# A fused attention and mixture-of-experts kernel: another order for VectorE's routing work inside the attention loop

## The chip, the cores and the metric

The kernel runs on one core of one Trainium2 chip. The core has five engines with a queue each: TensorE (PE in the profile; its weight loads are PEld), VectorE (DVE), ScalarE (ACT), GpSimd (POOL) and SyncE (SP), which here issues most of the transfers. Each engine works through its own instructions in the order in which they are written; the engines meet only at semaphores. The metric is the device time of one execution in microseconds (us), lower is better. The kernel before took 3224.88 us (median of 3 runs, 3223.79 to 3228.11).

## The reference: what is computed

The input x has 8 batches of 1024 tokens of 512 features. All of it is float32.

1. Attention. LayerNorm of x, without scale or shift. Each of 16 heads has 32 features. With xh the normalized row, the angles are `theta_q = xh / (1 + |w_q|) + b_q + t * phi_q`, likewise `theta_k`, and `theta_v = xh / (1 + |w_v|) + b_v`, where t is the place of the token. Q and K are `concat(cos theta, sin theta)` (64 wide), V is `cos theta_v + sin theta_v`. Sine and cosine come from a table of 2048 entries with linear interpolation. Then causal softmax attention per head, and `theta_out = out / (1 + |w_out|) + b_out`; what is added to x is `cos theta_out + sin theta_out`.
2. Mixture of experts. LayerNorm again; a router, `softmax(xn @ Wr + br)` over 8 experts; each token goes to its best two experts; each expert takes from each batch the first 160 (`int(1024 / 8 * 1.25)`) of the tokens that chose it, in order of token; later ones are dropped. Each expert is 512 -> 2048 (relu) -> 512, and the outputs, weighted by the router's probabilities, are added to x.

The router therefore needs, for every batch: the row statistics of x after attention, the normalized rows, their product with Wr, the two largest probabilities of each token, and a running count of the tokens of each expert, which gives a token its slot.

## The kernel before, in words

**The attention loop.** The loop at L1736 runs n from 0 to 31: batch b = n // 4, and chunk c = n % 4, which is 4 of the 16 heads (128 features). A chunk has two pairs of heads. For each pair, `scores` (L675) makes ten tiles of scores by matmuls (L684, with a causal mask added by matmuls, L698), and ScalarE takes the exponential of each (L704). `attend` (L710) multiplies the exponentials by V (L718), and VectorE scales the result into `av_sb` (L726). `turn` (L742) transposes that back to token order on TensorE (L216), and VectorE divides by the row sums (`rec` L753, `o_p` L755). `o_pre` and `o_post` (L643, L651) make the output angle (L647, L438), its sine, the sum with x in the tile `x_mid` (L658), and the statistics of that sum (`st_mid`, L661).

**Work for the next chunk in the same iteration.** While a chunk's scores and products run, the angles of the next chunk are made. `qk_pre` (L508) transposes the normalized input on TensorE (L216) and VectorE forms the q and k angles (`qk_f`, L525); `angle` (L437) makes `qk_r` from it (L438). `square` (L440, L442) and `absolutes` (L581, L585) are ScalarE's work on these. In the middle of the iteration ScalarE does a block of sines: a table load, cos (L594), `sine` (L445) of q and k, of v and of the output angle, and then `nc.scalar.activation(warm, split_c, AF.Exp)` (L1844), which brings the table for the exponential back. I call the time from one of these L1844 instructions to the next a stage; a stage is the second half of one iteration and the first half of the next one. `qk_post` (L599) multiplies on VectorE (L448, `qk_c` and `qk_r`, 128x2048 each) and sends the pairs for the next scores by SP (L609). `v_pre` and `v_post` (L619, L639) do the same for v (L626, L631, L438, then L448 into `v`).

**The bank pairs.** Every tile `ps_s` is one of three pairs of PSUM banks: a tile of scores, the transposes of `turn` and `qk_pre`, and what the router puts into PSUM. TensorE can write the next tile only when the last reader of the pair's previous content is done. Exponentials release a pair on ScalarE; copies and sums release one on VectorE.

**The router of a batch.** `router(b)` (L787) is a generator. It runs through the four chunks of the batch after b, one step at a time, by `next(route)` or by `route_on(slot)` (L1755), which does it only in the chunk of that number. For all batches but the last its steps are

- places and root: eight aggregations of `st_mid` (L798) and the inverse root of the variances (`inverse_root`, L355: 12 small instructions L361 to L369); in the same step rows 0 and 1: two tiles of 128 tokens normalized (`rows`, L811, L813) and sent to DRAM by SP (L819)
- for each pair of row tiles g = 0 to 3: features (TensorE transposes the rows, L216, VectorE copies them to `xT`, L838), the next two rows (L813, with the store of `x_mid` at L792 after the last), and sums (products with Wr, L875; VectorE copies them to `lg`, L880; sums over chunks by L858; VectorE adds br into `prob`, L882)
- choice: the largest logit and its subtraction (L926, L927), an empty step, the exponential on ScalarE (L930), then division (L932 to L934) and the two best experts (L941 to L948, once each), then the mask and the sums over row tiles (L954 to L957)
- counts: TensorE counts the tokens before each (L858 on `mask` and `prior`), and VectorE reads the counts (L966, L967)
- slots (L970 to L982), with scatters by POOL after them.

**What sets the order.** The engines PE, DVE, ACT and SP are scheduled by hand (L121): an engine's order is the order of the calls in the loop body. `with_asides(count)` (L1759) advances the tiles of scores by `count`, and each side generator in `asides` by one step per tile. `part(route)` (L988) is the router up to its next named step. `residual` is `o_post` of the chunk before the last. `begin` is true in the second half of an iteration with c == 0 and the first half of that with c == 1. Seven routers (batches 0 to 6) run in the loop; the eighth runs among the experts, from `ending` (L1886), and is not touched. After the loop, the experts take from about 1300 us to the end.

## Time and profile before

| what | value |
|---|---|
| median of 3 runs | 3224.88 us (3223.79 to 3228.11) |
| the profiled execution's own time | 3227.77 us |
| its span, first to last instruction | 3226.0 us |
| PE busy | 3114.4 us, 97% |
| DVE busy | 2309.3 us, 72% |
| ACT busy | 1680.1 us, 52% |
| mean granted TensorE clock | 0.992 |
| window 205 to 1280 us (seven batches with a router) | 1075.0 us, of them PE busy 1021.14, ACT 856.70, DVE 831.25 |

The profile is of one execution. Busy time of an engine is the union of its instructions. A wait names the instruction that waited and the one whose end released it, as inferred from semaphores; a line such as `L684` is a line of the kernel. PEclk is the part of TensorE's full clock that was granted. A matmul's end is modelled, so a busy PE need not be at its peak.

### The profile page before, as it was taken

Reading aid. Unit: us, or ns where it says so; the run is one execution under the profiler, and the core shown is the slowest. Engines: PE = TensorE matmul, PEld = TensorE weight load, DVE = VectorE, ACT = ScalarE, POOL = GpSimd, SP = SyncE. Lnnn points to the kernel's source line nnn. Section 1 sums busy time; section 2 is a strip of 40 time slices with the busy share of each in tenths; the row PEclk is TensorE's granted clock in tenths of the full one; section 3 lists DMA queues with packets and bytes.
Section 4 is the critical chain, followed back from the end, with each engine's and each line's share of the span. In section 5 each row is a group of like instructions: output and inputs, shape, how many; then the busy total and the mean of one; then the engine's idle time right before and its main releaser. Section 6 shows DMA issues by size and latency. Waiting matters only on the chain.

```text
span 3226.0 us, 52455 instructions
## 1 busy us (share of the span) xinstructions
PE 3114.4 (97%) x20086; PEld 2155.2 (67%) x20086; DVE 2309.3 (72%) x4808; ACT 1680.1 (52%) x2630; POOL 420.0 (13%) x387
## 2 busy tenths in 40 slices
PE   5999999999999999999999999999999999999998
PEld 2544444444444444578788688689699699698697
DVE  8887878787877776646767767767767668657665
ACT  7878888878787876413323323323423423423423
POOL 2000202020202022421101101100110110110010
PEclk9999999999999999999999999999999999999999
DMA  5435354444544443434414514513523523523421
GB/s 165 145 99 164 102 161 112 151 131 137 159 140 133 116 132 92 131 83 115 136 41 115 147 33 112 153 29 110 154 37 102 153 47 94 151 57 105 128 53 27
DMA packets 288554, 358.80 MB, mean 111 GB/s; under 512 B 28376, under 2 KB 199088, under 8 KB 276272
## 3 DMA queue, kind: packets, MB, share of 16 engines
q1 hardware_dynamic: 264944, 312.20, 32.9%
q0 software_dynamic: 22912, 43.22, 7.1%
q8 instruction: 160, 2.62, 0.3%
q14 instruction: 90, 0.74, 0.1%
q10 hardware_dynamic: 448, 0.02, 0.0%
HBM read 207.02 MB, written 81.22 MB: 89 GB/s over the span
## 4 chain that ended last, share of the span: by engine, by line
PE 73%; DVE 11%; ACT 11%; issue 3%; DMA 1%; another core or an unknown queue 0%; SPq 0%; POOLq 0%; ACTq 0%; POOL 0%; DVEq 0%
PE ps_p L1238 30%; PE ps_p L1474 10%; PE ps_p L1537 10%; PE av L718 8%; PE ps_p L1352 8%; PE ps_s L684 7%; ACT e L704 6%; PE ps_s L216 1%; DVE st_mid L661 1%; ACT qk_c L594 1%; DVE av_sb L726 1%; ACT t_r L445 1%; ACT qk_r L445 1%; DVE qk_f L525 1%; DVE x_mid L658 1%
## 5 line engine op out<-in xcount | busy, mean ns | idle before, releaser
L684 PE MATMUL ps_s<-qk 64*128 64x512 f32 (+3 forms) x3072 | 598.2, 513 | 64.7 <-ACT e L704 23.6
L704 ACT ACTIVATE e<-ps_s 128x1024 f32<-128x1024 f32 (+1 forms) x640 | 559.1, 943 | 114.4 <-PE ps_s L698 53.9
L718 PE MATMUL av<-e,v 128*64 128x512 f32 (+3 forms) x3072 | 509.5, 488 | 0.0
L684 PEld LDWEIGHTS ps_s<-qk 64*128 64x128 f32 x3072 | 267.2, 191 | 256.6 <-ACT e L704 102.5
L718 PEld LDWEIGHTS av<-e,v 128*64 128x64 f32 x3072 | 206.0, 137 | 278.8 <-issue 258.6
L1238 PE MATMUL ps_p<-xe_s,t 128*128 128x256 f32 (+1 forms) x1024 | 319.1, 434 | 6.5 <-ACT hid L1248 6.5
L1238 PE MATMUL ps_p<-xe,w 128*128 128x256 f32 (+1 forms) x1024 | 317.6, 433 | 1.1 <-issue 1.1
L1238 PE MATMUL ps_p<-xe,t 128*128 128x256 f32 (+1 forms) x1024 | 318.0, 433 | 0.0
L1316 POOL DMA_INDIRECT out_dram<-y,slots x80 | 127.2, 1590 | 1262.4 <-ACT y L1311 1008.1
L769 POOL DMA_INDIRECT slot_d<-token,slot x128 | 153.8, 1202 | 1055.3 <-issue 658.9
L1238 PEld LDWEIGHTS ps_p<-xe_s,t 128*128 128x128 f32 x1024 | 194.8, 191 | 88.6 <-ACT hid L1248 7.1
L1238 PEld LDWEIGHTS ps_p<-xe,t 128*128 128x128 f32 x1024 | 194.6, 190 | 80.9 <-issue 1.3
L1238 PEld LDWEIGHTS ps_p<-xe,w 128*128 128x128 f32 x1024 | 193.7, 190 | 79.4 <-issue 1.2
L1537 PE MATMUL ps_p<-w_t,hid 128*128 128x256 f32 x960 | 212.4, 379 | 0.8 <-DVE y L1590 0.8
L1281 DVE TENSOR_TENSOR hid<-hid 128x256 f32<-128x256 f32 (+1 forms) x128 | 63.4, 495 | 207.4 <-ACT hid L1279 203.7
L1537 PEld LDWEIGHTS ps_p<-w_t,hid 128*128 128x128 f32 x960 | 180.0, 190 | 24.4 <-DVE y L1590 1.2
L1238 PE MATMUL ps_p<-xe_s,w 128*128 128x256 f32 (+1 forms) x512 | 158.9, 433 | 0.6 <-ACT p L1254 0.6
L726 DVE TENSOR_SCALAR av_sb<-av,inv_o 128x512 f32<-128x512 f32 x128 | 94.8, 745 | 84.8 <-PE av L718 80.7
L1352 PE MATMUL ps_p<-w,hid 128*128 128x256 f32 x640 | 142.9, 379 | 0.0
L1474 PE MATMUL ps_p<-w,hid 128*128 128x128 f32 x1104 | 141.8, 275 | 0.0
L1311 ACT ACTIVATE y<-y,slots 128x256 f32<-128x256 f32 (+1 forms) x120 | 65.9, 578 | 143.5 <-DVE y L1389 105.5
L698 PEld LDWEIGHTS <-keys_b 64*128 64x128 bf16 x1536 | 79.1, 95 | 90.6 <-issue 72.2
(291 smaller groups left out, 5231.6 us busy)
## 6 DMA issues: line engine op xcount, KB each, us to landing
w<-in_L_ffn_W_dram SPq DMA_DIRECT2D x256, 256.0 KB
w<-in_L_ffn_W_dram SPq DMA_DIRECT2D x64, 512.0 KB
qk<-qk_c SPq DMA_DIRECT2D x124, 256.0 KB
qk<-qk_r SPq DMA_DIRECT2D x120, 256.0 KB
qk_base<-base_d SPq DMA_DIRECT2D x28, 1024.0 KB
xn_d<-xn SPq DMA_DIRECT2D x72, 256.0 KB
rows_d<-xg SPq DMA_DIRECT2D x70, 256.0 KB
x_mid<-in_L_attn_x_dram SPq DMA_DIRECT2D x16, 1024.0 KB
```

Source lines behind the costliest of these rows:

```text
L684: nc.tensor.matmul(ps[:, a, at : at + w], lhsT=pair[r, 1, kb * P : (kb + 1) * P], rhs=pair[r, 0, q0 : q0 + w], start=at == 0, stop=not own ...
L698: nc.tensor.matmul(out_, lhsT=keys_b[r, part, :], rhs=late, start=False, stop=part == 1, skip_group_check=True,)
L704: nc.scalar.activation(e, ps[:, :, :n], AF.Exp, scale=UNIT * UNIT / math.sqrt(2 * DH))
L718: nc.tensor.matmul(av[a * 64 : (a + 1) * 64, q0 - 512 * h :], lhsT=vt[:, kb, 2 * pr + a, :], rhs=es[i][:, a, at : at + w], start=kb == 0, ...
L726: nc.vector.tensor_scalar(av_sb, av, inv_o[:, q : q + 1], None, ALU.mult)
L769: queued = nc.gpsimd.indirect_dma_start(out=slot_d[b], out_offset=bass.IndirectOffsetOnAxis(ap=idx, axis=0), in_=src, in_offset=None,)
L1238: nc.tensor.matmul(ps, lhsT=weights[:, k, :], rhs=rows[:, k, :], start=first and k == 0, stop=last and k == 1, skip_group_check=True,)
L1311: nc.scalar.activation(part, part, AF.Identity, scale=meta[:, e, jj[r], 1:2].bitcast(F32))
L1316: ins = nc.gpsimd.indirect_dma_start(out=out, out_offset=bass.IndirectOffsetOnAxis(ap=meta[:, e, jj[r], 0:1], axis=0), in_=y, in_offset=No ...
L1352: nc.tensor.matmul(ps, lhsT=hid[:, k, part, cols], rhs=ws[weight][:, k, :], start=first and k == 0, stop=last and k == NHQ - 1, skip_group ...
L1474: nc.tensor.matmul(ps, lhsT=left[:, k, :], rhs=right[:, k, :], start=first and k == 0, stop=k == 3, skip_group_check=True,)
L1537: nc.tensor.matmul(ps[:, b * DC : (b + 1) * DC], lhsT=hid[:, k, part, b * P : (b + 1) * P], rhs=ws[weight][:, k, :], start=first and k == ...
```

## The change

Nothing is computed that was not computed before: each engine has as many instructions as before, and the orders of SP's transfers and of POOL's work are the same. The order of calls in the loop body is another one.

- Places, root and rows 0 and 1: they stood at the end of the iteration with c == 0, on VectorE ahead of `qk_f` and `qk_r` of the next iteration. They now stand in the iteration with c == 1, after `qk_r`.
- v in the iteration with c == 1: `v_post` stood right after `qk_r`, followed by `v_pre` of the next chunk. `v_post` now stands after features 0 and rows 2 and 3, and `v_pre` after rows 4 and 5. v's square on ScalarE stood after five of the ten tiles of scores; it now stands after the ten, directly ahead of the sines.
- Features 0: their transposes on TensorE stood ahead of the first tile of scores of c == 1, and stand behind it.
- Choice, in the iteration with c == 2: `residual` (`o_post`, L448, L658, L661) stood after the first best expert, and now stands ahead of the whole choice. The exponential L930 stood after four tiles of scores and now stands after eight. The division, the two best experts and the sums over row tiles stood ahead of `turn` and `o_pre`, and now stand behind them.
- Sums 2 in c == 1 and counts in c == 2: VectorE's part stood behind the second product of `qk_post` (L448, `qk_r`), and stands ahead of it.

```diff
         if more:
             angle(*qk_st)
         if begin:
-            v_post(n, v_st)
-            v_st = rest(v_pre(n + 1))
+            next(route)
         if n and n + 2 < NCK:
             load_base(n + 2)
...
                 rest(keep(place, both(qk_st)))
             for h in range(2):
                 rest(attend(n - 1, 1, h, es1[h], halves1))
-        for _ in range(2):
-            route_on(1)
         route_on(2)
         with_asides(1)
         route_on(2)
-        if c == 2 and route is not None:
-            asides.append(part(route))
+        for _ in range(2):
+            route_on(1)
+        if begin:
+            v_post(n, v_st)
+        choice = part(route) if c == 2 and route is not None else iter(())
+        if c == 2:
+            rest(residual)
         with_asides(4)
         rest(residual)
         for _ in range(2):
...
         if n == 0:
             rest(keep(place, both(qk_st)))
             v_st = rest(v_pre(1))
-        if n == 0 or begin:
             square(v_st[0])
+        with_asides(1)
+        next(choice, None)
+        with_asides(1)
+        route_on(1)
+        if begin:
+            next(route)
+            v_st = rest(v_pre(n + 1))
+        with_asides(1)
+        some(2, choice)
         with_asides(2)
-        for _ in range(2):
-            route_on(1)
-        with_asides(3)
         for g in asides:
             rest(g)
...
         if late:
             turn(1, halves1, pos)
             o_st = o_pre(n - 1, pos)
+        if begin:
+            square(v_st[0])
+        rest(choice)
         for _ in range(2):
             route_on(1)
...
             next(post)
         some(NTT, *products)
+        route_on(1)
+        route_on(2)
         next_pairs = rest(post) if more else None
 
         es1, halves1 = [[], []], []
         ahead = [scores(pairs[1], h, es1[h]) for h in range(2)]
-        route_on(1)
-        route_on(2)
         some(3, *ahead)
         begin = c == 0 and late
...
         if begin:
             route = router(b - 1)
-            next(route)
         some(2, *ahead)
         route_on(1)
```

## The prediction

> **What bounds the kernel now.** I read the page's shares first, then busy times by stage, then the waits, then the timeline where they fall. TensorE is busy 97% of the span and the experts (from 1300 us) show no gap, so only the attention loop can give anything. Busy time by stage (columns: stretch, length, then busy us of PE, PEld, DVE, ACT, POOL, then PE clock, DMA share, GB/s), for one batch without and with router work:

> ```profile
> PE 3114.4 (97%) x20086; PEld 2155.2 (67%) x20086; DVE 2309.3 (72%) x4808; ACT 1680.1 (52%) x2630; POOL 420.0 (13%) x387
> ...
> 329.01:363.98 34.97, 34.81 (x290) 17.40 (x286) 30.73 (x58) 31.60 (x34) 14.20 (x11) 1.00 0.38 91
> 363.98:406.08 42.10, 38.64 (x386) 19.30 (x384) 34.34 (x70) 31.95 (x33) 7.67 (x9) 1.00 0.50 144
> 406.08:446.72 40.64, 39.85 (x397) 20.44 (x387) 29.61 (x64) 32.52 (x34) 0.00 (x0) 1.00 0.53 164
> 446.72:486.15 39.43, 36.47 (x288) 17.88 (x284) 31.12 (x68) 31.91 (x33) 1.20 (x1) 0.96 0.46 134
> 521.51:565.12 43.61, 40.15 (x386) 19.54 (x384) 34.18 (x70) 32.08 (x34) 7.24 (x9) 0.96 0.48 139
> 605.77:643.51 37.74, 34.77 (x288) 17.28 (x284) 30.94 (x68) 31.74 (x34) 1.01 (x1) 1.00 0.47 140
> ```

> Call them stage 0 (no router), 1, 2 and 3. In stage 0 PE has 0.16 us idle in 34.97: there it is the bound. In stages 1, 2 and 3 it is idle for 3.46, 0.79 and 2.96 us. None of the engines is full there, so these are waits for order. PE's waits and ACT's longest wait in 200 to 1250 us (total, times, longest) name them:

> ```profile
> PE ps_s L684 <- ACT e L704: 19.4, 22, 1.8
> PE ps_s L684 <- DVE tmp L966: 14.5, 7, 2.1
> PE ps_s L684 <- DVE xT L838: 8.0, 7, 1.2
> PE ps_s L684 <- DVE prob L882: 5.1, 8, 0.7
> ...
> ACT qk_f L442 <- DVE qk_r L438: 101.8, 26, 7.7
> ```

> The timeline (start, us, engine) shows how stages 1 and 3 come to stand:

> ```profile
> 376.30 2.72 DVE L525 SCALAR_TENSOR_TENSOR qk_f<-ps_s,inv_qk,qk_base 128x512 int32<-128x512 f32 x4
> 381.17 2.19 ACT L442 ACTIVATE qk_f<-qk_f,split_c 128x1024 f32<-128x1024 uint16 x2 [7.36 <-DVE qk_r L438]
> ...
> 386.21 0.70 PE L684 MATMUL ps_s<-qk 64*128 64x256 f32 x4 [1.51 <-ACT e L704]
> 388.14 1.99 PE L684 MATMUL ps_s<-qk 64*128 64x512 f32 x8 [1.14 <-DVE xT L838]
> ...
> 447.77 2.28 DVE L448 SCALAR_TENSOR_TENSOR qk_r<-qk_f,qk_r 128x2048 f32<-128x2048 f32 x1
> 447.89 0.70 PE L684 MATMUL ps_s<-qk 64*128 64x256 f32 x4 [0.74 <-ACT e L704]
> 449.96 0.21 DVE L966 TENSOR_TENSOR tmp<-hot,ps_s 128x64 f32<-128x64 f32 x1
> 450.74 5.83 PE L684 MATMUL ps_s<-qk 64*128 64x512 f32 x18 [2.07 <-DVE tmp L966]
> ...
> 450.89:454.30 3.41, 3.41 (x10) 1.37 (x12) 3.34 (x5) 1.02 (x1) 0.00 (x0) 0.50 0.99 255
> ```

> VectorE reaches `qk_f` late because places, root and rows stand ahead of it (371.95 to 376.30). ACT, in order, cannot square q and k before 381.17, so its exponentials come late and PE waits 1.51; then PE waits for the pair that `xT` holds (1.14). In stage 3 PE waits for the pair with the counts, which VectorE reads only behind `qk_r`'s product. The last row is a stretch with the clock at 0.50, right behind that wait.

> **Stage 1, walked with the durations of this batch.** I keep every duration and change only the order; times are those of the profile.

> - qk: PE's transposes end at 373.18 (372.46 + 0.72), so `qk_f` starts at 373.24 instead of 376.30. From `qk_f`'s start to `qk_r`'s end it is 4.84 (376.30 to 381.14): `qk_r` ends at 378.0, 3.1 earlier. ACT's squares and absolutes take 4.0: done at 382.1 instead of 385.2.
> - places, root, rows 0 and 1: 4.35 (371.95 to 376.30), now 378.0 to 382.4. Waiting behind them on DVE: two `av_sb` (1.40), to 383.8, then `xT`. PE's products end at 381.98, its first tile of scores at 382.98, features' transposes at 383.5; DVE copies `xT` 383.8 to 385.1 (before: to 388.09).
> - PE: second tile to 384.6; third needs the first exponential (383.05 to 384.07): free; fourth needs `xT`: 385.1 against 388.14, 3.0 earlier. The moved rows' DMAs: rows 0 and 1 go to DRAM by SP when written (382.4), and rows 2 and 3 reuse their buffers at 385.1, 2.7 later; before, it was 11.6 (376.4 to 388.0). Where they land is in no row; if it takes longer than 2.7, DVE waits for the rest, and since `lg` behind it is ready only 0.2 ahead of PE's sixth tile, PE waits nearly as long: 0 to about 2 us, of which I take 0. SP's and POOL's orders are the same; behind these DMAs on SP stands the base load (issued at 379.04, now about 383), whose data are wanted at about 414. From the fourth tile to the next products it was 9.84 (388.14 to 397.98), and 9.6 without its small waits: products at 394.75, 3.2 earlier.
> - v: `v_post` (1.21, to 387.3) is needed at 394.75. `v_pre` (1.29 + 1.23 + 0.69) follows rows 4 and 5 and ends at 395.5. v's square writes in place and waits for that: ACT, done with the tenth tile at 394.2, stands 1.3 us, with the sines queued behind it. Square 1.15, sines with both table loads 8.5 (397.79 to 406.28): the exponential's table is back at 405.1, against 406.28. The square used to run between exponentials, where ACT had time; here it is on ACT's chain, paid out of the 3.2. If v's angle is 1 us later, the next stage's first exponential is 1 us later.
> - Start of stage 2: products end at 402.7, sums' matmuls to 403.4, three tiles to 406.0. `prob` (L882) is read ahead of `qk_r`'s product, at 404.9, so the wait of 0.64 is gone; the fourth tile waits for the first exponential, 406.1. It was 410.09. **4.0 us per batch so far.**

> **Stage 2 to 3.** (In chunk 2 of batch 0, without a router, `o_post` moves ahead too; DVE has idle time there, and I cost it at nothing.) PE is the bound in the rest of stage 2, so all moves up by 4.0; I walk in the old times. `o_post` (4.1) runs 428.55 to 432.7, then L926 and L927 to 433.15. L930 on ACT, behind eight tiles, runs at about 435: no wait. `turn`'s transposes end at 436.66; `rec` to the output angle takes 2.88 (441.37 to 444.25): to 439.6 instead of 444.3. So ACT's wait of 0.99 ahead of the output's sine is gone, and the table is back 1 us earlier. The choice then takes 2.17 (432.28 to 434.45) + 2.85 (438.52 to 441.37), to 444.6. PE gets to the counts at 444.49: **an added wait of about 0.2**, with the scores behind it. Then on DVE `av_sb` 0.66, `qk_c` 2.20, `av_sb` 0.66, L966 to L966 0.72: counts read at 448.85. The tile that waited until 450.74 starts at 448.9; the wait of 0.74 is gone. `qk_r` is 1 us later than if counts stayed behind, but its scores are a half iteration away. **1.8 us.**

> Sum of waits: (4.0 + 1.8) x 7 batches = 41 us.

> **The clock.** Of the seven stages 1, four show PEclk below 1, and of the seven stages 3, five. The same stage with and without: 43.61 against 42.10 (1.5 us) and 39.43 against 37.74 (1.7). 4 x 1.5 + 5 x 1.7 = 14.5 us. [...] I follow the row, and take two thirds, 10 us, since a stretch of 1.1 us (447.8 to 448.9) stays: ends 0 and 14.5.

> Bounds of the whole: nothing, if the waits only move; at most all PE idle of stages 1 to 3 (3.46 + 0.79 + 2.96 = 7.2, x 7 = 50) and the clock, 65 us. Taken: 41 + 10 = 51 of the profiled 3227.8, which is 2.9 above the median; from the median of 3224.9 that is **3174 us**.

> **Rivals.**
> - The waits go but the clock drops go on at other waits: 41, **3184**. For it: drops come in only some batches with the same waits. Against: less idle time to set them off.
> - The gain of stage 1 is given back at the sines, since v's angle stands behind rows 4 and 5 and ACT waits for it. If 2.5 of 4.0 go, (1.5 + 1.8) x 7 = 23 and half of the clock, 5: **3197**. For it: ACT's order has no way round the square. Against: stage 2's first exponential waited 1.59 for PE, so ACT has some room.
> - The change does nothing for PE: each wait is replaced by one as long. **3225**. Against: DVE is at 34.3 of 42.1 us, with idle time to use.
> - Slower: the load of `x_mid` in stage 2. `o_post` needs it at 435.71 now, at 429.8 - 4.0 = 425.8 then. The DMA share is 1.02, 1.03 and 0.98 in 403:409, 409:418 and 418:427 and 0.05 after, so the load lands by about 427, and starts 1.8 earlier with the store ahead of it: 425.2, just in time. If it is d late, DVE's choice and L930 are late; ACT has 2 us, and past that the last exponentials and the sines wait with it. With 8 us (5.8 and the clock) to lose, it decides at d = 10; at d = 12 it costs 2 x 7: **3239**.

> **Chances.** As worked 0.52, clock stays 0.18, given back 0.16, nothing 0.04, slower 0.10. The sum is the likeliest, not a mean. A range of 3160 to 3203 holds the first three, with the greater clock gain at its low end. A measurement here can tell 0.2% (6.4 us) from no change: faster 0.86, within 0.04, slower 0.10.

> **What would show it.** Right: stage 1 near 41 us, stage 2 near 37 (its end moves with ACT's sines, 1 us more than PE), stage 3 near 37, the three together near 115 to 117 instead of 122.2; no wait of PE for `xT` (8.0) or `prob` (5.1); that for L966 from 14.5 to about 8; ACT's wait of 7.36 ahead of q's square near 4; a new wait of ACT for v's angle near 1.3; PEclk of 1.00 in most stages. Wrong: PE waits longer than 1 us at the counts, ACT's new wait over 2.5 us, or DVE standing at rows 2 and 3 or at L658 for a transfer.

## The result, and the profile after

The changed kernel takes 3179.84 us (median of 4 runs, 3179.05 to 3180.82), the kernel before beside it 3224.38 us: a ratio of 0.986 (95% interval 0.9843 to 0.9877). The forecast was 3174 us. The profiled execution of the changed kernel has a span of 3177.3 us, against 3226.0.

The first row is from the page; the others are the table of stretches of the changed kernel (length, then busy us of PE, PEld, DVE, ACT, POOL, then PE clock, DMA share, GB/s). The stages are those of the batch shown in the prediction: stages 0, 1, 2 and 3 in order, then the longest stage 1 of the seven.

```profile
PE 3096.0 (97%) x20086; PEld 2147.3 (68%) x20086; DVE 2310.1 (73%) x4808; ACT 1676.5 (53%) x2630; POOL 420.6 (13%) x387
...
318.96:354.21 35.25, 35.09 (x296) 17.60 (x290) 31.03 (x58) 31.79 (x34) 13.92 (x11) 1.00 0.36 90
354.21:396.20 41.99, 40.49 (x402) 20.27 (x398) 35.48 (x73) 32.19 (x33) 7.88 (x9) 1.00 0.51 151
396.20:432.93 36.73, 36.50 (x355) 18.61 (x353) 26.53 (x61) 31.92 (x35) 0.00 (x0) 1.00 0.56 174
432.93:470.01 37.08, 36.22 (x298) 18.46 (x294) 32.62 (x68) 31.85 (x34) 1.21 (x1) 1.00 0.48 143
809.22:855.68 46.46, 42.39 (x402) 20.86 (x398) 35.26 (x73) 32.29 (x33) 7.68 (x10) 0.96 0.58 170
```

PE's idle in stage 1 fell from 3.46 to 1.50 us, in stage 2 from 0.79 to 0.23, in stage 3 from 2.96 to 0.86. Stages 1 to 3 of this batch take 115.8 us together, against 122.2. A stage is cut where ScalarE ends its sines, so a gain of PE in stage 1 shows mostly in stage 2: over seven batches stage 1 lost 3.0 us in all, stage 2 27.0 and stage 3 13.0. The longest stage 1 has 4.07 us of idle, and its clock is 0.50 for 3.41 us (837.66 to 841.07).

The waits of the changed kernel in 200 to 1250 us (total, times, longest):

```profile
ACT qk_f L442 <- DVE qk_r L438: 89.2, 26, 4.9
DVE xn L813 <- DMA xn_d<-xn: 12.2, 10, 3.1
ACT v_p L442 <- DVE t_r L438: 8.6, 13, 0.9
...
PE ps_s L684 <- DVE tmp L966: 5.0, 7, 0.7
PE ps_s L684 <- DVE lg L880: 4.4, 6, 1.0
PE ps_s L684 <- ACT e L704: 3.9, 9, 0.5
PE ps_s L216 <- DVE xn L813: 2.6, 3, 1.0
PE ps_s L684 <- DVE xT L838: 1.5, 3, 0.6
PE ps_s L684 <- DVE prob L882: 0.7, 1, 0.7
```

PE's four large waits (19.4, 14.5, 8.0 and 5.1) are now 3.9, 5.0, 1.5 and 0.7. Two are new: for `lg` and for the rows of L813, 7.0 us together. The second row shows what is behind them: VectorE stands 12.2 us at L813, for the store that still reads the row tile's buffer. That is the wait that the prediction had bounded at 0 to 2 us and taken at 0.

The timeline of the batch at 354 us (start, us, engine), in the places that the prediction showed:

```profile
364.19 2.73 DVE L525 SCALAR_TENSOR_TENSOR qk_f<-ps_s,inv_qk,qk_base 128x512 int32<-128x512 f32 x4 [1.93 <-PE ps_s L216]
368.98 2.19 ACT L442 ACTIVATE qk_f<-qk_f,split_c 128x1024 f32<-128x1024 uint16 x2 [4.93 <-DVE qk_r L438]
375.96 1.99 PE L684 MATMUL ps_s<-qk 64*128 64x512 f32 x8 [0.50 <-DVE xT L838]
376.05 0.55 DVE L813 TENSOR_SCALAR xn<-x_mid,mv,rstd 128x512 f32<-128x512 f32 x1 [0.23 <-DMA xn_d<-xn]
377.28 0.55 DVE L813 TENSOR_SCALAR xn<-x_mid,mv,rstd 128x512 f32<-128x512 f32 x1 [0.69 <-DMA xn_d<-xn]
379.35 1.99 PE L684 MATMUL ps_s<-qk 64*128 64x512 f32 x8 [0.19 <-DVE lg L880]
...
436.02 0.22 DVE L966 TENSOR_TENSOR tmp<-hot,ps_s 128x64 f32<-128x64 f32 x1
436.29 1.56 PE L684 MATMUL ps_s<-qk 64*128 64x512 f32 x6 [0.62 <-DVE tmp L966]
436.41 2.28 DVE L448 SCALAR_TENSOR_TENSOR qk_r<-qk_f,qk_r 128x2048 f32<-128x2048 f32 x1
```

The wait of 1.51 for an exponential is gone, `xT` costs 0.50 instead of 1.14, and the counts are read ahead of `qk_r`'s product: the tile behind them stands 0.62, where it stood 0.74 and 2.07.

### The profile page after: what moved, and what is told of

The parts are those of the page before. It is cut to its first block, busy times and chain, and to the rows that moved or that the text cites. A ratio compares the mean times of both kernels' runs of the same rounds, so it can differ in the third digit from the quotient of the medians.

```text
span 3177.3 us, 52455 instructions
## 1 busy us (share of the span) xinstructions
PE 3096.0 (97%) x20086; PEld 2147.3 (68%) x20086; DVE 2310.1 (73%) x4808; ACT 1676.5 (53%) x2630; POOL 420.6 (13%) x387
## 4 chain that ended last, share of the span: by engine, by line
PE 78%; ACT 11%; DVE 7%; issue 2%; DMA 2%; SPq 0%; another core or an unknown queue 0%; POOLq 0%; POOL 0%; ACTq 0%; DVEq 0%
PE ps_p L1238 30%; PE ps_p L1474 10%; PE ps_p L1537 10%; PE ps_s L684 9%; PE av L718 9%; PE ps_p L1352 8%; ACT e L704 6%; PE ps_s L216 1%; ACT qk_c L594 1%; DMA xn_d<-xn 1%; ACT t_r L445 1%; ACT qk_r L445 1%; PE ps_s L698 1%; ACT L594 1%; DVE qk_f L525 1%
## 5 line engine op out<-in xcount | busy, mean ns | idle before, releaser
L684 PE MATMUL ps_s<-qk 64*128 64x512 f32 (+3 forms) x3072 | 584.1, 502 | 33.5 <-DMA qk<-qk_r 12.5
L704 ACT ACTIVATE e<-ps_s 128x1024 f32<-128x1024 f32 (+1 forms) x640 | 555.1, 944 | 85.6 <-PE ps_s L698 46.2
L684 PEld LDWEIGHTS ps_s<-qk 64*128 64x128 f32 x3072 | 261.4, 187 | 219.6 <-ACT e L704 93.1
L1537 PEld LDWEIGHTS ps_p<-w_t,hid 128*128 128x128 f32 x960 | 180.0, 190 | 24.4 <-DVE y L1590 1.2
```

The lines of the kernel that those rows point to most:

```text
L684: nc.tensor.matmul(ps[:, a, at : at + w], lhsT=pair[r, 1, kb * P : (kb + 1) * P], rhs=pair[r, 0, q0 : q0 + w], start=at == 0, stop=not own ...
L704: nc.scalar.activation(e, ps[:, :, :n], AF.Exp, scale=UNIT * UNIT / math.sqrt(2 * DH))
L1537: nc.tensor.matmul(ps[:, b * DC : (b + 1) * DC], lhsT=hid[:, k, part, b * P : (b + 1) * P], rhs=ws[weight][:, k, :], start=first and k == ...
```

## The experiments

My theory: the gain is PE's idle time that the change removes in stages 1 to 3, and the half-clock stretches that this idle had set off; what is missing from the forecast is the wait for the stores of rows. The rivals: one part makes the gain alone (stage 2 lost 27 us, which points at the choice); rows and counts work only together; the clock goes by something else than these idles.

All runs are compared by one account. The loop is measured from the start of the first stage 1 to the last of the L1844 instructions (205.60 to 1280.67 us before). Its length less PE's busy time is the idle; the half-clock time is counted in stretches of 3.41 us. For the kernel before, the changed one and the one called best below, the row of the loop reads:

```profile
205.60:1280.67 1075.07, 1021.21 (x9040) 510.69 (x9034) 830.96 (x1665) 856.78 (x890) 145.04 (x129) 0.98 0.47 134
```

```profile
203.60:1235.76 1032.16, 1006.25 (x9040) 505.32 (x9034) 829.62 (x1665) 853.32 (x890) 144.33 (x129) 1.00 0.49 140
```

```profile
205.60:1224.77 1019.17, 1003.16 (x9040) 503.71 (x9034) 828.72 (x1665) 852.60 (x890) 140.62 (x129) 1.00 0.49 142
```

PE has the same 9040 instructions in each; 1075.07 - 1021.21 = 53.86 us is idle before, 25.91 after, 16.01 in the last.

| kernel | time, us | ratio to before (95%) | loop | PE idle | half-clock stretches |
|---|---|---|---|---|---|
| before | 3224.4 | 1 | 1075.1 | 53.9 | 10 |
| changed | 3179.8 | 0.9860 (0.9843 to 0.9877) | 1032.2 | 25.9 | 1 |
| rows_only | 3212.3 | 0.9955 (0.9938 to 0.9972) | 1070.0 | 45.0 | 14 |
| choice_only | 3216.8 | 0.9971 (0.9961 to 0.9981) | 1063.2 | 47.1 | 5 |
| counts_only | 3196.8 | 0.9908 (0.9892 to 0.9925) | 1043.4 | 39.8 | 1 |
| rows_back | 3202.0 | 0.9933 (0.9916 to 0.9950) | 1050.3 | 35.6 | 7 |
| prob_back | 3185.9 | 0.9875 (0.9856 to 0.9895) | 1037.6 | 30.0 | 2 |
| counts_back | 3191.9 | 0.9894 (0.9874 to 0.9914) | 1039.8 | 32.0 | 1 |
| rows_buf | 3172.3 | 0.9837 (0.9820 to 0.9853) | 1027.0 | 21.5 | 1 |
| v_first | 3177.1 | 0.9847 (0.9831 to 0.9863) | 1025.0 | 20.7 | 0 |
| reads_3 | 3173.8 | 0.9868 (0.9853 to 0.9883) | 1032.5 | 25.9 | 2 |
| reads_5 | 3180.4 | 0.9888 (0.9873 to 0.9903) | 1045.6 | 30.7 | 7 |
| square_mid | 3212.9 | 0.9992 (0.9983 to 1.0000) | 1071.1 | 50.3 | 14 |
| best | 3162.6 | 0.9833 (0.9819 to 0.9846) | 1019.2 | 16.0 | 0 |

The ratios are to the kernel before on the same chip: 3224.8 us beside the three single parts and rows_buf, 3226.0 beside the three kernels ending in _back and v_first, 3215.9 beside the last four. In these last four the part behind the loop is 5 to 10 us shorter; compare them with the others by ratio and by loop. A half-clock stretch costs about 1.7 us (measured below). With that, the change of idle plus 1.7 per stretch gives the change of the loop to within 3.5 us for every kernel but one (-28.0 - 9 x 1.7 = -43.3 for the changed kernel, measured -42.9). The exception, square_mid, is 7 us off: idle that lies inside a stretch at half clock is counted twice, which may be the reason; that is not shown.

### One part alone

rows_only, on the kernel before (places, root, rows, and v with its square):

```diff
         if begin:
-            v_post(n, v_st)
-            v_st = rest(v_pre(n + 1))
+            next(route)
...
-        for _ in range(2):
-            route_on(1)
         route_on(2)
         with_asides(1)
         route_on(2)
+        for _ in range(2):
+            route_on(1)
+        if begin:
+            v_post(n, v_st)
...
+        route_on(1)
+        if begin:
+            next(route)
+            v_st = rest(v_pre(n + 1))
...
+        if begin:
+            square(v_st[0])
```

> One part alone: places, root and rows behind q and k's angle, v's angle spread over the iteration with its square beside the sines; choice and counts as before. Theory A (the prediction's steps: stage 1's waits are PE's own, worth 4.0 us in each of 7 batches, and the clock of stage 1 comes back, 4 x 1.5): 3224.4 - 28 - 6 = 3190; no wait of PE for xT in L838 beyond 1 to 2 us in all, and half-clock stretches in stage 3 stay (5 of 7). Theory B (stage 1's marks moved by only 3 us in all and stage 2's by 27, so the gain is made by the choice behind the output's sum, not by the rows): 3218 to 3224. Theory C (rows and counts act only together, because a gain of stage 1 is lost again at the counts' wait): 3205 or more.

choice_only, on the kernel before:

```diff
-        if c == 2 and route is not None:
-            asides.append(part(route))
+        choice = part(route) if c == 2 and route is not None else iter(())
+        if c == 2:
+            rest(residual)
         with_asides(4)
...
         with_asides(1)
+        next(choice, None)
...
         with_asides(1)
+        some(2, choice)
...
+        rest(choice)
```

> One part alone: in stage 2 the output's sum and statistics go ahead, and the choice is spread behind them; rows, v and counts as before. Theory A (this part only takes away ACT's wait of 0.99 ahead of the output's sine and, alone, moves the counts later): 0 to 7 us faster, 3217 to 3224. Theory B (stage 2's 27 us are made here): 3197 or less. A slower result would come from counts that are late: PE waiting for them over 1 us in stage 3.

counts_only, on the kernel before:

```diff
         some(NTT, *products)
+        route_on(1)
+        route_on(2)
         next_pairs = rest(post) if more else None
...
-        route_on(1)
-        route_on(2)
         some(3, *ahead)
```

> One part alone: the counts and their reading ahead of q and k's product; all else as before. Theory A (removes the tile's wait for L966 of 2.07 and the 0.74 ahead of it, in which the last idle of about 1 stays: 1.8 us in 7 batches, and 5 half-clock stretches of stage 3 at 1.7): 3224.4 - 12.6 - 8.5 = 3203; PE's total for L966 from 14.5 to 5 to 8, the half-clock stretches of stage 1 stay. Theory B (the waits go, the half-clock stretches stay at other places): 3212. Theory C (the product is the later one by as much as was won, and its scores wait): 3220 to 3226.

The size of the parts is not the one that I gave them. The rows, which I held for two thirds of the gain, make 12.5 us alone (against 3224.8), the choice 8.0 and the two lines of the counts 28.0. That stage 2 got shorter does not mean that the choice did it: the choice alone takes 7.7 us from stage 2, and counts and choice without the rows (rows_back, below) 14.0 of the 27.0.

For rows alone, theory C has the time (3205 or more) and the coupling right, but not the place: the wait at the counts stays as it was, and the gain is lost at `prob`. PE's waits:

```profile
PE ps_s L684 <- DVE tmp L966: 14.5, 7, 2.1
PE ps_s L684 <- DVE prob L882: 11.4, 8, 3.1
```

and the place with the longest:

```profile
877.20 0.33 PE L698 MATMUL ps_s<-later_b,keys_b 64*128 64x128 bf16 x4
880.66 0.70 PE L684 MATMUL ps_s<-qk 64*128 64x256 f32 x4 [3.12 <-DVE prob L882]
```

The wait for `xT` is gone (0.9 in all), but PE comes to the start of stage 2 earlier and stands there for `prob`, which VectorE still reads behind `qk_r`'s product: 11.4 us instead of 5.1. Part of what the rows win is lost 20 us later. On top of it all seven stages 3 have half-clock stretches, four of them twice as long (14 stretches against 10), with the same idle of 0.74 and 2.07 as before.

Counts alone removed 14.1 us of idle (theory A: 12.6), though PE's wait for L966 fell only to 10.4, where A had 5 to 8. They removed nine stretches instead of five, also in stage 1, whose idle of 1.4 to 1.6 and 1.15 stood unchanged. So the number of stretches is not a matter of the idle's length alone; this is taken up below.

### One part undone

rows_back is the kernel before with the edits of choice_only and counts_only together, so the changed kernel without its first part.

> The changed kernel with the first part undone: places, root, rows and v as before; choice and counts as changed. The first four runs gave a way to count: time of the loop = PE's work + PE's idle + about half of the time at clock 0.50. Theory A (count by idle): per batch 0.45 + 1.50 + 1.15 stay in stage 1 and 0.6 to 0.7 in stage 3, against 1.6 in the changed kernel's undisturbed batches, but without its 7 us of waits behind the stores of rows: 8 us more idle, and 0 to 5 half-clock stretches of stage 1 at 1.7, 3188 to 3197. Theory B (the prediction's sizes: the rows are worth 28 and 6): 3214. Theory C (a half-clock stretch follows where a window of 3.41 us, on a grid fixed within an execution, has 1.7 us or more of idle): every half-clock stretch of this run starts on one grid of 3.41, and behind windows with 1.7 or more.

prob_back, on the changed kernel:

```diff
-        route_on(1)
         route_on(2)
         next_pairs = rest(post) if more else None
...
+        route_on(1)
         some(3, *ahead)
```

> The changed kernel with one of the two moved lines undone: stage 2's sum, prob (L882), is read behind q and k's product again; the counts stay ahead of it. Theory A (this line, not the counts, is what rows alone lacked: there PE stood 11.4 us for prob): PE's wait for L882 is 7 to 20 us in all, 3188 to 3196. Theory B (the prediction's size, 0.64 in 7 batches): 3184. Theory C (no matter for PE): 3180.

counts_back moves the other of these two lines back (`route_on(2)`) and leaves `route_on(1)`.

> The changed kernel with the other moved line undone: the counts are written and read behind q and k's product again; prob stays ahead of it. Theory A (count by idle): 1.80 (choice alone) to 2.81 (before) of idle in stage 3 against 0.65, 8 to 15 us, and 0 to 7 half-clock stretches at 1.7, 3188 to 3206, PE's wait for L966 10 to 15 us. Theory B (with the choice late, the counts' place no longer matters): 3180 to 3183. Half-clock stretches, if any, on one grid of 3.41 us behind windows with 1.7 or more of idle.

In place, the rows are worth 18.2 us of the loop (1050.3 - 1032.2): 9.7 of idle and six stretches. Theory A had the idle right (8) and the stretches too low (7 in the run), so the time lies above its range; B's 34 is refuted. `prob`'s line is worth 5.4 and the counts' 7.6. PE's wait for L882 is 8.1 us in prob_back, in the range that A gave, and 0.7 with the line in place; the time, 3185.9 from two runs 7.7 us apart, is below A's range and between the two theories; the 0.64 per batch of the prediction is what the old order showed, not what leaving the line would cost in the new order. For the counts, A holds at its lower end: PE's wait for L966 is 10.6. The choice was not undone by itself in the full change, so what it is worth there is not known.

### The stores of rows

rows_buf, on the changed kernel (`bufs=3` also stands at the two other places that use these buffers, not shown):

```diff
-            xn = row2.tile([P, D], F32, name="xn2")
+            xn = row2.tile([P, D], F32, name="xn2", bufs=3)
...
+        work = row2.tile([P, 2 * P], F32, name="lg", bufs=1)
+        quarter = [
+            work[:, i * NTT * E : (i + 1) * NTT * E].rearrange("p (t e) -> p t e", e=E)
+            for i in range(4)
+        ]
...
-            oh = t3(f"hot_{k}")
+            oh = quarter[k]
...
-        mask, prior = t3("mask"), t3("prior")
+        mask, prior = quarter[2:]
```

> The changed kernel with three buffers instead of two for the router's row tiles; to make room, the tiles hot, mask and prior of the choice lie in the buffer of lg, and nothing else is changed. Theory A (rows 2 and 3 wait for the stores of rows 0 and 1; 12.2 us of VectorE, of which PE stands for L813 2.6 and for L880 4.4, and the one half-clock stretch of stage 1 hangs on it): 3179.8 - 7 - 1.7 = 3171, L813's wait for its store gone or under 2 us, PE's waits for xn and lg under 2 us together. Theory B (PE stands at this place for something else that is as late, the exponentials or features): 3177 to 3180 with the wait for the store gone. Theory C (the shared buffer adds a wait): above 3182.

v_first, on the changed kernel:

```diff
-        for _ in range(2):
-            route_on(1)
+        route_on(1)
         if begin:
             v_post(n, v_st)
+        route_on(1)
```

> The changed kernel with v's product (L448 into v, 1.21 us of VectorE) between features and rows 2 and 3 instead of behind rows 2 and 3; two buffers. Theory A (the stores of rows 0 and 1 need 2 to 3 us and the product covers 1.2 of it): VectorE's wait of L813 for stores from 12.2 to 3 to 6 us, PE's waits for L813 and L880 together from 7.0 to 2 to 4, 3173 to 3177. Theory B (rows 2 and 3 are late by the product instead, and PE's sixth tile waits for lg as long): 3179 to 3183.

In both, theory A has the cause right. The three lines are VectorE's wait for the stores in the changed kernel, in rows_buf and in v_first:

```profile
DVE xn L813 <- DMA xn_d<-xn: 12.2, 10, 3.1
```

```profile
DVE xn L813 <- DMA xn_d<-xn: 4.7, 3, 2.6
```

```profile
DVE xn L813 <- DMA xn_d<-xn: 3.1, 4, 1.1
```

PE's waits for L813 and L880 fall from 7.0 to 2.1 and to 0.2. I had expected under 2 us to remain of VectorE's wait in rows_buf; 4.7 did, since a third buffer serves row 2, and row 3 still takes row 0's. The half-clock stretch that was to go with the wait is still there in rows_buf and is gone in v_first. The loop is 5.2 and 7.1 us shorter. The intervals of the times overlap with each other and with that of the changed kernel; it is the waits and the loop that tell them apart.

### v's square

square_mid, on the changed kernel:

```diff
             v_st = rest(v_pre(n + 1))
+            square(v_st[0])
         with_asides(1)
...
-        if begin:
-            square(v_st[0])
```

> The changed kernel with v's square right behind v's angle, among the last exponentials, instead of beside the sines. Theory A (beside the sines it lies on ACT's chain with 1.15 and the wait of 0.9, and the middle has room): 1 to 2 us per batch faster, 3168 to 3175. Theory B (in the middle ACT stands for the angle, ready at 386.7 in the batch at 354 us, with three exponentials queued behind that were done by 385.9): PE waits for L704 with the products, 2 to 3 us per batch slower, 3194 to 3203.

Nearly the whole gain is gone (ratio 0.9992). The two lines are the waits that took its place:

```profile
PE ps_s L216 <- ACT e L704: 34.0, 34, 4.6
ACT v_p L442 <- DVE t_r L438: 32.8, 13, 4.8
```

ScalarE stands up to 4.8 us for v's angle, three exponentials are queued behind it, and PE stands for the bank pairs that they hold. Theory B holds, with twice its price: 24.4 us of idle, and 13 more half-clock stretches, which B had left out. So, with v's angle spread behind the rows, the square has to go behind the exponentials. The rival "given back at the sines" is answered by the changed kernel itself: there the wait is at most 0.9.

### The clock

In the kernel before, the half-clock stretches of the loop start at 229.02, 450.89, 546.46, 703.48, 768.33, 925.34, 1020.92, 1085.77 and 1242.78 us; the first is 6.83 us long, the others 3.41, and the granted clock in them is 0.50. One unit fits all the starts, 3.4133 us (1013.76 us from the first to the last, over 297): in it they stand at 0, 65.00, 93.00, 139.00, 158.00, 204.00, 232.00, 251.00 and 297.00 from the first. Below, a window is one such unit, on the grid that the stretches of an execution fix. How much idle in a window goes ahead of half clock, these starts do not say. Two kernels ask this, both from the changed kernel:

```diff
         for k in range(TOPK):
-            TT(tmp, hot[k], place, ALU.mult)
+            for _ in range(3 if k else 1):
+                TT(tmp, hot[k], place, ALU.mult)
```

> The changed kernel in which VectorE does each of the two reads of the counts (L966, 0.25 us from one to the next) three times, with the same result: PE's idle ahead of the tile that waits for them grows by 1.0, from 0.65 to 1.65 in one piece in each of 7 batches. Theory A (a half-clock stretch needs 1.7 us of idle in one window of the 3.41 us grid): no stretch at 0.50 in stage 3, cost 7 us, 3187. Theory B (any idle piece of over about 1 us can set it off): 4 to 5 stretches in stage 3, 3195.

reads_5 has 5 in place of 3.

> The same with five times each: idle 2.65 in one piece, nothing else changed. Theory A (1.7 us in one window of the grid): the two parts of 2.65 are both under 1.7 only where a window's border falls in the middle 0.75 of it, so about 78% of the stages, 5 to 6 of 7 (or all or fewer, where a batch is near a whole number of windows long), are followed by 3.4 us at 0.50: 14 + 5.5 x 1.7 = 23, 3203. [...]

The edit repeats only the second of the two reads (`if k`), not each of them as I had written: two and four more reads, 0.25 us from one to the next, not four and eight. So the idle came to 1.24 and 1.84 us (1.75 of it in one piece), not 1.65 and 2.65, and the times that the theories gave are too high. The question is answered all the same: reads_3 has no stretch in stage 3 (theory B, any piece of over about 1 us, had 4 to 5); reads_5 has five in seven (theory A had 5 to 6, for an idle of 2.65), and in its other two batches a border cuts the idle. Windows of the grid in reads_5: an idle of 1.84 that lies in one window and the window after it, then the idle of a batch in which a border cuts it:

```profile
284.27:287.68 3.41, 1.57 (x20) 1.05 (x18) 3.17 (x11) 2.10 (x3) 0.00 (x0) 1.00 0.45 86
287.68:291.09 3.41, 3.41 (x10) 1.39 (x10) 3.38 (x3) 1.02 (x1) 0.00 (x0) 0.50 0.98 231
...
745.07:748.48 3.41, 1.89 (x22) 1.11 (x18) 3.24 (x8) 2.54 (x3) 0.00 (x0) 1.00 0.36 70
748.48:751.89 3.41, 3.09 (x14) 1.46 (x16) 3.34 (x5) 1.85 (x3) 0.00 (x0) 1.00 0.95 214
```

and in reads_3, where the whole of its 1.24 lies in one window:

```profile
284.97:288.38 3.41, 2.17 (x12) 1.08 (x12) 3.24 (x8) 1.67 (x3) 0.00 (x0) 1.00 0.84 166
288.38:291.79 3.41, 3.41 (x28) 1.73 (x26) 3.34 (x5) 3.41 (x5) 0.00 (x0) 1.00 1.05 262
```

With five reads stage 3 takes 39.8 us where the stretch comes and 38.1 where it doesn't: 1.7 us for one stretch, between batches that do the same. I then took every window of the grid in 200 to 1250 us at full clock with at least 0.9 us of idle, in the twelve kernels that have a stretch to fix the grid by. Of those with 1.9 us or more, 35 of 35 are followed by half clock; of 1.7 to 1.9, 10 of 13; of 1.45 to 1.7, 4 of 30; below 1.45, none of 44. The 1.7 of theory A was written down before rows_back, counts_back and these two kernels ran. So in these traces the windows with and without half clock behind them part between 1.45 and 1.9 us of idle. The seven that 1.7 puts on the wrong side may come of the modelled ends of matmuls; this is not shown.

This fits what the single parts showed. Stage 3 of the kernel before has 0.74 and 2.07 us of idle within 3.6 us, and five of its seven batches have a stretch behind it. Of the two without one, the first is cut by a border into 1.66 and 1.15 us (the windows from 290.46 and 293.87); the other has 1.89 us in one window (from 607.90) and is among the seven. In rows_only the stretches of stage 3 start 46, 47, 46, 47, 46 and 46 windows apart, and all seven batches have one. In counts_only it is 44.9 to 45.4 windows from one stage 1 to the next, and its idle of about 1.5 and 1.15 us is cut by a border so that at most 1.71 us lie in one window in six of seven batches; the seventh, with about 2.1, has the stretch. Where the borders fall can outweigh a gain: rows_back is counts_only with the choice added and has 4.2 us less idle, but its loop is 6.9 us longer, since stage 1, with the same idle in both (21.1 and 21.2 us up to stage 2's fourth tile), has seven stretches in place of one. Of the 44 windows with 0.9 to 1.45 us of idle none was followed by half clock.

### The best of these

best is rows_buf and v_first together, with both reads of the counts ahead of their reductions:

```diff
         for k in range(TOPK):
-            TT(tmp, hot[k], place, ALU.mult)
-            nc.vector.tensor_reduce(spot[:, :, k], tmp, AX.X, ALU.add)
+            TT((tmp, prob)[k], hot[k], place, ALU.mult)
+        for k in range(TOPK):
+            nc.vector.tensor_reduce(spot[:, :, k], (tmp, prob)[k], AX.X, ALU.add)
```

> Three changes on the changed kernel together: three buffers for row tiles (hot, mask and prior in lg's), v's product ahead of rows 2 and 3, and both reads of the counts ahead of their two reductions (the second into prob's tile). Theory A (idle adds up): the waits for the stores of rows go wholly (7 us of PE and the one half-clock stretch), and the wait for L966 falls by one reduction, 0.25 in 7 batches: 3166 to 3172. Theory B (VectorE is late with lg whatever the order of what is ahead of it): 3172 to 3177.

It took 3162.6 us on its chip, a ratio of 0.9833 (0.9819 to 0.9846), which would be 3170.5 of the 3224.4 (theory A: 3166 to 3172). Its loop is 13.0 us shorter than that of the changed kernel, 9.9 of it idle, with no stretch left. PE's wait for the counts is 2.5 us in all instead of 5.0. The waits for the stores are not wholly gone, as theory A had it: VectorE still stands 3.6 us for them, and PE 1.1 for L813. The interval just touches that of the changed kernel; by time alone the two are not told apart for certain, by the loop they are.

## Why the prediction was right or wrong

The direction and the range were right; 3174 is 5.8 us too low. That it came so near is in part luck: two errors of opposite sign.

| term | predicted | measured |
|---|---|---|
| stages 1 and 2, 7 batches | 28 | 21 |
| stage 3, 7 batches | 13 | about 15 |
| waits for stores of rows | 0 | -7 |
| idle together | 41 | 28.0 |
| half-clock stretches | 10 | 15.3 |
| sum | 51 | 43, the loop 42.9, the medians 44.5 |

The first measured term is PE's idle from its qk transposes to stage 2's fourth tile, over seven batches: 25.7 us before, less the 4.4 in best, where little of the wait for the stores is left. The third is what the changed kernel has there above best (11.3 - 4.4); PE's waits for L813 and L880 come to 7.0 as well. The second is about 2.15 of the batch at 354 us, times 7. The idle is the loop's (53.9 - 25.9), which the three terms miss by 1; the stretches are 9 x 1.7.

- **Stage 1 to 2, 4.0 per batch: right for the new order as such, not reached in the changed kernel.** From PE's qk transposes to stage 2's fourth tile the batch walked takes 37.63 us before, 34.68 in the changed kernel (2.95 less) and 33.77 in best (3.86 less), which differs between these two marks only in the buffers of rows and the place of v's product. The starts are, in this order:

```profile
372.46 0.72 PE L216 MATMUL ps_s<-ident,xn 64*128 64x64 f32 x16
410.09 1.97 PE L684 MATMUL ps_s<-qk 64*128 64x512 f32 x8
...
362.69 0.71 PE L216 MATMUL ps_s<-ident,xn 64*128 64x64 f32 x16
397.37 2.04 PE L684 MATMUL ps_s<-qk 64*128 64x512 f32 x8
...
363.82 0.71 PE L216 MATMUL ps_s<-ident,xn 64*128 64x64 f32 x16
397.59 2.04 PE L684 MATMUL ps_s<-qk 64*128 64x512 f32 x8
```

  The first step went as worked out in five of the seven batches: `qk_f` begins 0.04 to 0.08 us behind the transposes' end (I had 0.06), `qk_r` ends 2.9 to 3.5 earlier, and ScalarE's wait is 4.1 to 4.4. The batch walked is one of the two others: there `qk_f` begins 0.79 us behind, `qk_r` ends 2.4 earlier, and ScalarE waits 4.93. Most of what lacks over the seven batches is the next term. In idle alone best wins 3.0 per batch, not 3.9; PE's busy time there falls too (34.0 to 33.4 us in the batch walked), and why is not shown.
- **The stores of rows, 0 to 2 with 0 taken: wrong.** In the batch walked VectorE waits only 0.23 and 0.69. In the batch at 809 us it waits 3.06 and 0.81, PE stands 2.9 us in three pieces, and the clock falls to 0.50 for 3.41 us (837.66 to 841.07). This batch belongs to both tensors in DRAM that the experts read (`REACH`, L67), so each of its rows is stored twice (L816 to L819), and the stage has more traffic (DMA share 0.58 against 0.51). The stores of rows 0 and 1 in the batch walked, then in this one, and the wait behind them:

```profile
372.87 1.07 SPq L819 DMA_DIRECT2D xn_d<-xn  x2
...
827.14 1.93 SPq L819 DMA_DIRECT2D xn_d<-xn  x4
...
833.77 0.55 DVE L813 TENSOR_SCALAR xn<-x_mid,mv,rstd 128x512 f32<-128x512 f32 x1 [3.06 <-DMA xn_d<-xn]
```

  The mechanism was written down; at the middle of its bound, 1 us, the term would have been 7. rows_buf and v_first take most of the wait away and win 4.4 and 5.2 us of idle.
- **Products 3.2 earlier, v's square, the sines:** the products come 2.13 earlier in the batch walked and 3.03 in best, for the reasons above. ScalarE's wait for v's angle is 0.87, not 1.3, and nothing is given back at the sines.
- **Stage 3, 1.8 per batch: right in mechanism, a little low.** The counts add no wait of PE in the batch walked. Of the 1.1 us of idle that I left standing 0.6 to 0.7 is left, so 2.1 to 2.2 are won.
- **`x_mid`, the slower rival:** VectorE waits for that load once, 1.0 us. The mechanism hardly came into play.
- **The clock, 10 of 14.5: mis-sized, on the right side.** Nine of ten stretches went. The rival with the clock unchanged gave 3184, which is nearer to the time (4.2 us) than my 3174 (5.8); but in it the clock gives nothing and the waits 41, and both are refuted. No run shows the two thirds of 14.5 that I took, which was my estimate; the runs showed nine stretches of about 1.7 us gone, 15.3. What I followed held: in five of seven batches of the kernel before half clock came behind 0.74 and 2.07 us of idle within 3.6 us, and by the windows above behind all 35 with 1.9 us or more in one window.
- **What stage lengths were to show:** stages 2 and 3 are mostly 36.7 and 37.1 as said; stage 1 is 41.6 to 43.3 and once 46.5, where I said 41. No wait of PE over 1 us at the counts, and PEclk of 1.00 in 20 of 21 stages. VectorE standing at rows 2 and 3 was on my list of what would be wrong, and it was there.

The rest of the profiled difference (48.7 against 42.9 in the loop) lies outside the loop: 2.0 us ahead of the first L1844 and 3.8 behind the last. Kernels with and without each part fall on either side of both (first mark near 97 or 99 us), so I count neither to the change.

## What to carry to other kernels

Measure a reordering between two fixed points of the engine that sets the pace, in several batches and not in one, and then ask of each buffer that is reused sooner what still reads it: here a store that had 11.6 us to land before and about 3 in the changed kernel (372.87 to 376.05) became a wait, 12.2 us of VectorE in all. The parts of this reordering did not add up: with the rows alone PE's wait for `xT` fell from 8.0 to 0.9 us and that for `prob` rose from 5.1 to 11.4, so judge a part by undoing it in the full change, too. Count the clock by windows: in these traces half clock followed all 35 windows of 3.41 us with 1.9 us or more of idle and none of 44 with 0.9 to 1.45, whether the idle was in one piece (1.75 us of the 1.84 in reads_5) or in two (0.74 and 2.07).
